# A graph layer and a two-expert feed-forward: the expert stage put into a hand-written order, with the turning of a later group behind layer two

## The chip, the cores and the metric

One NeuronCore of a Trainium2 chip runs the whole program. The metric is the time of one execution on the device in microseconds (us). Its engines are named as in the profile: PE multiplies matrices (PEld is its loading of weights), DVE and ACT are the vector and the scalar engine, POOL is GpSimd, and SP issues transfers (SPq is its queue of instructions). Each engine has its own list of instructions; a semaphore holds an instruction back until another engine, or a transfer, has done what it needs.

## The reference

The input is `x` with 6250 rows of 256 numbers, and a list of 206,250 edges. A graph convolution with a residual comes first; behind it stands the part that matters here, a layer norm and a feed-forward of two experts out of eight, chosen once for all rows:

```python
x = x + gnn(layernorm(x), edges)
# feed-forward on xf = layernorm(x), shape (6250, 256)
h = gelu(einsum('nd,edf->enf', xf, W1) + b1)      # 256 -> 512, exact gelu
y = einsum('enf,efd->end', h, W2) + b2            # 512 -> 256
out = einsum('ne,end->nd', w_dense, y)            # two experts have weight, top_k = 2
out = layer_norm(out + xf, gamma, beta)
x = x + out
```

## The kernel before

The 6250 rows lie in 49 tiles of 128 rows. The first two thirds of the time are the graph convolution; it ends with `x1_d`, the rows before the second layer norm, in device memory, and with the mean and the reciprocal deviation of each row, `mean2` and `rstd2`. A router then picks the two experts and loads their weights (`w1_sb`, `w2_sb`; `w2_sb` and the second bias are scaled by the routing weights on DVE, lines 1231 to 1238).

The stage of the experts goes over 13 **groups**: group 0 has one tile, the twelve others have four (`TN = 4`). A group passes through these steps:

- `take(i)` (line 888) allots three tiles and issues one transfer on SP (line 898), 512 KB of `x1_d` into `xt`. The tiles `yt` and `xt` come from a pool with `AH + 3` = 6 buffers each, `xT2` from one with `AH + 1` = 4; `AH = 3`.
- `turn(i, ps_x, eng)` (line 903) normalizes: for each of the four tiles one instruction (line 910, on DVE for groups 3 and up) writes `yt` from `xt`, and two PE transposes (line 915) put it into the PSUM tile `px`. Two ACT copies (line 917) take `px` to `xT2`.
- `biases(i)` (line 919) adds the second bias to `yt` and `beta` to `xt`, two POOL instructions (lines 922 and 925).
- `layer_1(i)` (line 1252) makes eight tiles `p1` in PSUM (two experts, four blocks of 128 hidden units), each by matmuls over the two halves of 256 columns (line 1261; each shows as two PE instructions, 32 for a group), and ACT takes each through gelu into `hT` (line 1265). `ps_1` has three buffers for `p1`.
- `layer_2(i)` (line 1269) makes, for each of the four tiles, one `p2` over both experts (line 1282; 16 PE instructions for a tile, 64 for a group). Behind it stands a chain on DVE and ACT for the tile: add `yt` (line 1287), the statistics of the last layer norm (1288, 1289), add epsilon (1291), square root on ACT (1292), subtract and scale by gamma (1294), reciprocal (1297), scale and add `xt` (1298). SP then stores the tile (line 1301).

Up to the stage, `take`, `turn` and `biases` have already run for groups 0, 1 and 2. In the stage ten turns are left, those of groups 3 to 12.

What sets the order: the part of the program under `tc.manual_schedule(engines={PE, DVE, ACT, SP, POOL})` (the convolution, and line 930 on, up to the scaling of the weights) has each engine's instructions in the order in which they are written. The stage of the experts, from line 1244, is not under it: there a planner in the framework puts each engine's instructions into an order of its own when the program is built, and may set an instruction ahead of those written before it on the same engine. The written order of the stage is

```python
        layer_1(0)
        for i in range(len(groups)):
            if i + 1 < len(groups):
                layer_1(i + 1)
            if i + AH < len(groups):
                take(i + AH)
                turn(i + AH, ps_x, nc.vector)
                biases(i + AH)
            layer_2(i)
```

## Time and profile before

| | us |
|---|---|
| three runs: median (lowest to highest) | 1150.8 (1148.29 to 1150.85) |
| the profiled execution | 1151.31 |
| its span, first to last instruction | 1149.2 |
| PE busy in the span | 1090.8 (95%) |
| DVE, ACT, POOL busy | 721.5, 623.1, 539.0 |
| PE busy from 795.60 to 1149.20, a stretch of 353.60 | 346.02 |
| DVE, ACT, POOL busy in that stretch | 129.56, 116.63, 56.00 |

The span is what lies between the first and the last instruction of the execution; the 2.1 us between 1149.2 and 1151.31 lie around it. "Busy" is the time in which an engine works on an instruction. The stage of the experts fills the last third of the span, from about 786 us. In the rows of the timeline a bracket at the end says how long the engine stood idle ahead of the row, and what ended that. The column PEclk is the clock that PE was granted, as a share of the full one.

### The profile page before, as it was taken

How to read it: one execution, taken by the hardware profiler on the slowest of the kernel's cores; microseconds unless marked ns; L12 is line 12 of the kernel's file. 1: busy time of each engine (PE TensorE's matmuls, PEld its weight loads, DVE VectorE, ACT ScalarE, POOL GpSimd, SP SyncE). 2: the span in 40 equal slices, each digit the busy share in tenths (PEclk: the TensorE clock that was granted, in tenths of full speed). 3: DMA queues.
4: the chain of work that ended last, by engine and by line, in shares of the span. 5: the costliest groups of instructions: out<-in, count | busy, mean ns of one | idle time of the engine just before them, and what ended most of it. 6: DMA issues, size and time to landing. Idle time of an engine off the chain costs nothing. (4 is left out here: it accounts for less than half of the span.)

```text
span 1149.2 us, 17869 instructions
## 1 busy us (share of the span) xinstructions
PE 1090.8 (95%) x6552; PEld 836.3 (73%) x6552; DVE 721.5 (63%) x1523; ACT 623.1 (54%) x1529; POOL 539.0 (47%) x473
## 2 busy tenths in 40 slices
PE   6977999999999999999999999885999999999997
PEld 5766788878888888788888888763566666666666
DVE  6878876867777877777777778745333333322335
ACT  3786466766766666676667666522533333333330
POOL 3713246777767676777666766425411111100000
PEclk9997899999999999999999999886999999999999
DMA  8709637676767777677777777534011111100001
GB/s 261 237 24 343 196 86 198 160 189 172 196 172 185 179 174 182 176 180 180 184 177 177 180 182 174 140 92 140 23 37 37 37 37 37 37 19 18 19 19 37
DMA packets 102750, 152.04 MB, mean 132 GB/s; under 512 B 10047, under 2 KB 48671, under 8 KB 102655
## 3 DMA queue, kind: packets, MB, share of 16 engines
q0 software_dynamic: 54080, 99.35, 35.3%
q1 hardware_dynamic: 45378, 48.93, 13.0%
q10 hardware_dynamic: 3196, 2.55, 0.8%
q8 instruction: 53, 0.87, 0.3%
q14 instruction: 43, 0.34, 0.1%
HBM read 123.42 MB, written 27.37 MB: 131 GB/s over the span
## 5 line engine op out<-in xcount | busy, mean ns | idle before, releaser
L737 POOL DMA_INDIRECT rows<-hl_d,g_src x360 | 409.5, 1137 | 221.7 <-PE pg L775 104.6
L644 PE MATMUL po<-hp,a_t 128*128 128x512 f32 x1911 | 481.8, 402 | 0.8 <-ACT a_t L628 0.8
L644 PEld LDWEIGHTS po<-hp,a_t 128*128 128x128 f32 x1911 | 351.9, 190 | 70.2 <-ACT a_t L628 1.0
L628 ACT CAST a_t<-pa 128x392 fp32r<-128x392 f32 x624 | 257.8, 502 | 218.0 <-PE pa L624 216.5
L455 DVE TENSOR_TENSOR unit<-iota,loT 128x2048 bf16<-128x2048 bf16 x156 | 190.4, 1221 | 51.3 <-PE pa L624 51.3
L1261 PE MATMUL p<-xT,w_sb 128*128 128x512 f32 (+2 forms) x416 | 173.0, 577 | 1.6 <-ACT xT L917 1.6
L1282 PE MATMUL p<-w_sb,hT 128*128 128x256 f32 (+1 forms) x784 | 171.2, 379 | 0.0
L1282 PEld LDWEIGHTS p<-w_sb,hT 128*128 128x128 f32 (+1 forms) x784 | 147.9, 190 | 20.8 <-issue 0.9
L624 PEld LDWEIGHTS <-unit 128*128 128x128 bf16 x2496 | 124.1, 100 | 49.0 <-issue 24.8
L624 PE MATMUL pa<-unit 128*128 128x98 bf16 x2496 | 148.6, 212 | 9.5 <-DVE unit L455 5.6
L455 DVE TENSOR_TENSOR unit<-iota,keyT 128x1568 bf16<-128x1568 bf16 x156 | 150.8, 967 | 0.0
L1261 PEld LDWEIGHTS p<-xT,w_sb 128*128 128x128 f32 x416 | 79.6, 200 | 88.2 <-issue 82.9
L1287 DVE TENSOR_TENSOR yt<-yt,p 128x256 f32<-128x256 f32 (+1 forms) x49 | 20.6, 421 | 179.6 <-PE p L1282 179.6
L756 ACT ACTIVATE oh_g<-iota_f,g_dst 128x128 fp32r<-128x128 f32 x360 | 123.9, 423 | 0.0
L1265 ACT ACTIVATE hT<-p,b_sb 128x512 f32<-128x512 f32 (+2 forms) x104 | 67.3, 660 | 82.9 <-PE p L1261 82.7
L775 PE MATMUL pg<-rows,oh_g 128*128 128x512 f32 x360 | 106.0, 392 | 1.6 <-DMA rows<-hl_d,g_src 1.6
L1292 ACT ACTIVATE rs<-rs 128x1 f32<-128x1 f32 (+1 forms) x49 | 9.9, 203 | 150.0 <-DVE rs L1291 150.0
L925 POOL TENSOR_TENSOR xt<-xt,beta_bc 128x1024 f32<-128x1024 f32 (+1 forms) x13 | 29.5, 2274 | 130.0 <-DVE yt L910 130.0
L775 PEld LDWEIGHTS pg<-rows,oh_g 128*128 128x128 f32 x360 | 68.1, 189 | 18.4 <-DMA rows<-hl_d,g_src 3.7
L922 POOL TENSOR_TENSOR yt<-yt,b_sb 128x1024 f32<-128x1024 f32 (+1 forms) x13 | 29.6, 2273 | 89.7 <-PE px L915 80.4
L758 ACT ACTIVATE oh_g<-oh_g 128x384 fp32r<-128x384 f32 (+1 forms) x140 | 67.1, 479 | 4.4
L679 DVE RECIPROCAL rstd<-rstd 128x1 f32<-128x1 f32 (+1 forms) x49 | 8.0, 164 | 88.2 <-ACT rstd L678 88.2
(183 smaller groups left out, 777.1 us busy)
## 6 DMA issues: line engine op xcount, KB each, us to landing
hl_d<-hp SPq DMA_DIRECT2D x7, 1792.0 KB
x_d<-x SPq DMA_DIRECT2D x49, 128.0 KB
xt<-x_d SPq DMA_DIRECT2D x12, 512.0 KB
out_dram<-yt SPq DMA_DIRECT2D x48, 128.0 KB
rows<-hl_d,g_src POOLq DMA_INDIRECT x360, 3.8
xb<-in_x_dram SPq DMA_DIRECT2D x6, 896.0 KB
xs<-in_x_dram SPq DMA_DIRECT2D x39, 128.0 KB
xg<-in_x_dram SPq DMA_DIRECT2D x9, 128.0 KB
```

Source lines behind the costliest of these rows:

```text
L455: nc.vector.tensor_tensor(oh, iota2[:, :m, :].unsqueeze(1).to_broadcast([P, HG // 2, m, 2]), v[:, s].rearrange("p (q t) -> p q t", t=2).un ...
L624: nc.tensor.matmul(pa[:, i].rearrange("p j h -> p (j h)"), oh_lo[:, q, :, t], oh_key[:, q, :, t], start=True, stop=True,)
L628: nc.scalar.copy(tiles[n][:, :, b * 2 * BG : (b + 1) * 2 * BG], pa.rearrange("p i j h -> p h (i j)"),)
L644: nc.tensor.matmul(pouts[n].rearrange("p k d -> p (k d)"), tiles[n][:, g, :], hp2[g // TB][:, g % TB].rearrange("p k d -> p (k d)"), start ...
L737: nc.gpsimd.indirect_dma_start(out=g_rows[j], out_offset=None, in_=hl_d, in_offset=bass.IndirectOffsetOnAxis(ap=g_src[:, j // GC, j % GC : ...
L756: nc.scalar.activation(oh[:, i, :], iota_f, AF.Abs, bias=g_neg[:, g, c : c + 1])
L758: nc.scalar.activation(oh, oh.bitcast(F32), AF.Relu, scale=-1.0, bias=1.0)
L775: nc.tensor.matmul(pouts[n].rearrange("p k d -> p (k d)"), oh[:, i, :], g_rows.pop(g * GC + c), start=False, stop=(c == GC - 1),)
L922: nc.gpsimd.tensor_tensor(yt[:, :nt, :], yt[:, :nt, :], b2_sb.unsqueeze(1).to_broadcast([P, nt, D]), OP.add)
L1261: nc.tensor.matmul(p1[:, :cols], w1_sb[:, e, k, f * P : (f + 1) * P], xT[:, k, :cols], start=(k == 0), stop=(k == ND - 1),)
L1265: nc.scalar.activation(hT[:, e, f, :cols], p1[:, :cols], AF.Gelu, bias=b1_sb[:, e, f : f + 1])
L1282: nc.tensor.matmul(p2[:r], hT[:, e, f, t * P : t * P + r], w2_sb[:, e, f, :], start=(e == 0 and f == 0), stop=(e == TOP_K - 1 and f == NF ...
```

## The change

The pools get one more buffer each (7 for `yt` and `xt`, 5 for `xT2`), the stage is put under the manual schedule for all five engines, the transfer of a group is issued one iteration earlier, and the turning and the biases stand behind `layer_2` in place of ahead of it.

```diff
-    xp = ctx.enter_context(tc.tile_pool(name="xp", bufs=AH + 3))
+    xp = ctx.enter_context(tc.tile_pool(name="xp", bufs=AH + 4))
...
-        xT = hp.tile([P, ND, TN * P], F32, name="xT2", bufs=AH + 1)
+        xT = hp.tile([P, ND, TN * P], F32, name="xT2", bufs=AH + 2)
...
     with ExitStack() as ph:
+        ph.enter_context(tc.manual_schedule(engines={PE, DVE, ACT, SP, POOL}))
         op_ = ph.enter_context(tc.tile_pool(name="op", bufs=3))
...
+        take(AH)
         layer_1(0)
         for i in range(len(groups)):
             if i + 1 < len(groups):
                 layer_1(i + 1)
+            if i + AH + 1 < len(groups):
+                take(i + AH + 1)
+            layer_2(i)
             if i + AH < len(groups):
-                take(i + AH)
                 turn(i + AH, ps_x, nc.vector)
                 biases(i + AH)
-            layer_2(i)
```

## The prediction

> **What bounds the kernel now.** I read the chain of work that ended last first, in the stretch of the stage. Columns: start, length, engine and line, how many instructions.

> ```profile
> 795.68 17.60 PE p L1261 x52
> 813.28 0.76 PE px L915 x7
> 814.04 3.46 PE p L1282 x16
> 817.50 13.73 PE p L1261 x32
> 831.23 0.87 PE px L915 x8
> 832.11 13.81 PE p L1282 x64
> 845.92 13.73 PE p L1261 x32
> ```

> From 795 us on the chain is PE alone, and piece follows piece without a hole: layer one 13.73 us, the eight transposes of a turn 0.87, layer two 13.81 to 13.82, so 28.42 a group. The clock is granted in full from 799 us to the tail. So no reordering of the other engines can gain anything in the steady part; it can only open holes in PE's row. PE's order is already the written one (layer one of the next group, turn, layer two).

> The second view is the timeline of DVE at a line 910 and around the end of a layer two (at 845.92).

> ```profile
> 824.55 1.38 DVE L910 TENSOR_SCALAR yt<-xt,mean,rstd 128x256 f32<-128x256 f32 x4 [4.61 <-DMA xt<-x_d]
> ...
> 845.96 0.42 DVE L1287 TENSOR_TENSOR yt<-yt,p 128x256 f32<-128x256 f32 x1 [1.18 <-PE p L1282]
> 846.42 0.43 DVE L1288 BATCH_NORM_STATS2 st<-yt 128x6 f32<-128x256 f32 x1
> ...
> 847.56 0.16 DVE L1297 RECIPROCAL rs<-rs 128x1 f32<-128x1 f32 x1
> 847.75 0.49 DVE L1298 SCALAR_TENSOR_TENSOR yt<-yt,rs,xt 128x256 f32<-128x256 f32 x1
> ```

> The chain of the group's last tile ends at 848.24, which is 2.32 us after PE has left layer two. Line 910 runs elsewhere: twelve of them between 794 and 811 us (the turns of groups 3, 4 and 5), the four at 824.55 belong to group 6, while PE turns group 4 only at 831. The planner keeps DVE two turns ahead of PE, and its 4.61 us wait for the transfer holds up nobody.

> The third view is PE's timeline where the stage begins.

> ```profile
> 785.81 2.93 PE L1261 MATMUL p<-xT,w_sb 128*128 128x128 f32 x12 [1.65 <-ACT xT L917]
> 795.21 0.48 PE L915 MATMUL px<-ident_r,yt 128*128 128x128 f32 x1 [6.47 <-DVE yt L910]
> 795.48 4.93 PE L1261 MATMUL p<-xT,w_sb 128*128 128x128 f32 x22
> ```

> The planner put one transpose of group 3 into the middle of layer one of group 0. Its DVE instruction stood behind the scaling of `w2_sb`, so PE stood idle for 6.47 us with 20 of group 0's 32 matmuls and all of group 1's behind it. It also shows that PE does not pass a waiting transpose.

> **What it adds: a wait at each turn.** In written order DVE's list is: the chain of all four tiles of group i, then line 910 four times for group i+3. PE's list is layer two of i, the eight transposes, layer one of i+2. The transposes need line 910, line 910 stands behind the chain of the last tile, and that chain needs the last matmul of layer two. Queued behind the transposes is all of layer one. Counted from layer two's end at 845.92: chain ends +2.32 (848.24), gap to the next DVE instruction 0.05 (as between other rows), four line 910 at 1.38 to 849.67, 0.05 from DVE to PE (795.16 to 795.21 in the chain), the last pair of transposes 2 × 0.87 / 8 = 0.22, so layer one starts at 849.94 in place of 845.92 + 0.87 = 846.79 by the chain. That is 3.15 us; reckoned by issue (layer one's first matmul shows at 845.76 already, its weights drawn ahead) it is 3.31. I take 3.3, bounds 3.1 and 3.6 (transposes at half clock: a pair took 0.69 at 782 us). Ten turns: 33 us.

> **What the wait does to the clock.** Steps of the granted clock lie at 768.25, 788.73, 792.14 and 798.97, all multiples of 3.41 us apart, so I cut PE's time at that grid (window: length, PE busy, clock).

> ```profile
> 112.89:116.30 3.41, 1.94 (x28) 1.00 1.03 376
> 116.30:119.72 3.42, 2.48 (x29) 0.50 1.03 381
> 232.36:235.77 3.41, 2.46 (x11) 1.00 0.77 183
> 730.70:734.12 3.42, 0.00 (x0) 1.00 0.70 164
> 734.12:737.53 3.41, 3.17 (x22) 0.50 0.19 59
> 737.53:740.94 3.41, 3.41 (x10) 0.50 0.00 0
> ```

> A window with 1.94 us of work is followed by half clock, one with 2.46 is not, and it comes back after a full window only: 3.17 us did not do. The new hole lasts from layer two's end to 4.0 us later, with only scattered transposes in it; however the grid lies, one window has at least 2 us of hole, so I expect the clock to fall at every turn. If the grid cuts the hole φ after its start, and φ is over 1.4, the clock falls there, the next window holds the rest of the hole and is not full, and the third brings it back at φ + 6.83; PE works at half speed from 4.0 to then and loses (φ + 2.8) / 2, 2.1 to 3.1 us. With φ below 1.4 it falls a window later and loses 1.4 to 1.7. A group then takes 28.42 + 3.3 + loss; at a loss of 2.4 that is 34.13, ten windows, so φ stays where it is (1.9), and from another φ each turn brings it halfway there. I take 2.4 a turn, 24 us for ten; the bounds are 0 (the clock is full now, so it can't gain) and 3.1.

> [...]

> **What it removes.** The early transpose of group 3 leaves layer one of group 0: PE goes on at 788.74, and the 20 matmuls (0.215 each by 52 in 17.60 less 32 in 13.73) end at 793.0, so layer one of group 1 ends at about 806.8 in place of 813.28: minus 6.5 us. Bounds 0 (expert 1's `w1_sb`, whose landing the trace does not show, comes as late as the second bias at 792.05 and the rest of the start slips with it) and 6.5; the weights were issued ahead of that bias at 779 to 780 us at some 350 GB/s, so I take 6.5. DVE's wait for `xt` (4.61 us in this row) goes too, but no one waited for it.

> **What is moved at no cost, and its cover.** *SP:* ten transfers of 512 KB as before, 0.4 us of issue each, now ahead of the group's four stores; SP waits on line 1298 for most of the stage, and a transfer that landed within some 4 us has over 50 us before its turn. Without that cover: 4.6 us a turn. Two transfers, not three, now run beside the weights. *ACT:* the two copies (1.07 us) stand behind the four square roots and end at about 851.2, the first `p1` of the next layer one is ready at 851.9, table load 1.28 and gelu 0.69 end at 853.8; PE needs that buffer for its fourth `p1`, three times 1.72 after 849.94, at 855.1. Cover 1.3 us, and more at half clock; without it, its excess is paid at each turn. *POOL:* the two additions (2.35 us each) run in layer one, when DVE is idle; next to POOL's work at 794 to 811 twelve line 910 took 16.57 us, four of them 5.5 in place of 1.38, so without that cover a turn would wait 4.1 us longer. The buffers add no instruction. The tail (layer two of groups 11 and 12, the last chain, the store) is unchanged.

> **Sum.** Against the profiled execution, 1151.3 (span 1149.2 and 2.1 around it, 0.5 above the median): 33 + 24 − 6.5 = +50.5, so 1202.

> **Rivals.**
> 1. *The stall without the clock.* If the short transposes count as work and windows of over 2 us still hold the clock: 1151.3 + 33 − 6.5 = 1178. For it: 2.46 us was enough at 232.36. Against: the hole leaves 1.4 us or less in its worse window. 10%.
> 2. *The start gives nothing back.* Stall and clock as above, expert 1's weights late: 1208. With 3.6 and 3.1 a turn besides, 1218. 8%.
> 3. *The other side: DVE is not held.* If line 910 still gets ahead of the last chain, transposes find `yt` ready, only the start's gain remains: 1151.3 − 6.5 = 1145. This decides as soon as the wait and the clock together cost under 0.65 us a turn. For it: line 910 needs nothing from layer two. Against: under the same schedule the router's DVE and PE rows (941, 945, 953, 969; 948, 956, 1215, 915) stand in written order throughout. 3%.
> 4. *The change does not do what it says* (the planner's order survives, early transpose included): 1151. 2%.

> **How the numbers follow.** The forecast has 77%, with its own range 1193 to 1210 (a loss of 1.5 a turn, or no gain at the start). The range 1180 to 1211 leaves out most of rival 1, the far end of rival 2, and 3 and 4. A measurement here tells about 0.3% from no change: faster 3%, within 2%, slower 95%.

> **What would show it.** Right: in each of ten groups PE idle some 2.8 us ahead of line 915, released by DVE line 910, whose four rows start right behind a line 1298; clock 0.50 for one or two windows after it; starts of layer one 34 us apart; no 6.47 us wait at 789. Wrong: line 910 ahead of line 1287 in DVE's row (rival 3), spacing of 31.7 us (rival 1), or ACT, not DVE, releasing PE.

## The result and the profile after

Slower: 1187.05 us median of four runs (1185.05 to 1190.03) against 1150.82 (1148.29 to 1151.28), a ratio of 1.0322 with a 95% interval of 1.0293 to 1.035. The profiled execution took 1190.03, its span is 1187.8, 38.6 us over the span of before.

The waits of PE in the stage come first (releaser, us in total, times, longest), then the chain that ended last over two turns.

```profile
PE px L915 <- DVE yt L910: 27.9, 10, 2.8
```

```profile
865.78 13.83 PE p L1283 x64
879.63 0.43 DVE yt L1288
...
881.42 0.48 DVE yt L1299
882.38 1.32 PE px L915 x8
883.70 13.73 PE p L1262 x32
897.43 13.83 PE p L1283 x64
...
914.03 1.57 PE px L915 x8
915.59 15.07 PE p L1262 x32
```

(Lines from 1246 on have moved down by one to three: layer one's matmul is line 1262, layer two's 1283, the last chain's ends are 1288 and 1299.) The chain was PE alone before; now it leaves PE at the end of each layer two, runs through the whole DVE chain of the last tile and through line 910, and comes back to the transposes. Layer two is as long as before. Layer one is 13.73 us in one group and 15.07 in the next. The timeline of DVE at the turn of group 4 shows what the transposes wait for:

```profile
848.17 0.48 DVE L1299 SCALAR_TENSOR_TENSOR yt<-yt,rs,xt 128x256 f32<-128x256 f32 x1
848.57 1.37 DVE L910 TENSOR_SCALAR yt<-xt,mean,rstd 128x256 f32<-128x256 f32 x4
```

Line 910 starts as line 1299 ends, with no bracket of idle time. Its transfer was no hindrance: SP issued it before 786 us. Only the place of line 910 in DVE's list is late. PE's first transpose follows at 849.12.

Where the 38.6 us went, by the chain's rows of before and after:

| | us |
|---|---|
| ten holes from layer two's end to layer one's start (4.78, 4.33, 4.09, 4.33, six of 4.08 to 4.09), 42.1, less ten turns of 0.87 | +33.4 |
| layer one over 13.73 (0.50, 1.37, 1.34, three of 1.70; four of none) | +8.3 |
| start: layer one of group 0 to the end of layer one of group 1, 785.81 to 813.28 before, 789.48 to 810.05 after | −6.9 |
| up to the start of the stage, where the program is the same: 785.81 to 789.48 | +3.7 |

The last row is no part of the change. In the profiled executions of the experiments below, but for the sixth, which alters the start, layer one of group 0 starts anywhere from 784.5 to 788.8 us, and 1190.03 is the slowest of the four runs. Without that row the sum is 34.8; the medians differ by 36.2, and the 1.4 us between the two stay unexplained.

Of the first row some 1.2 us belong to the clock: at three turns (holes of 4.78, 4.33 and 4.33 in place of 4.08) the transposes ran at half clock. So the wait by itself cost 32.2 us, and the clock 9.5, of which layer one lost 8.3.

The third view is PE's time cut at the grid on which this execution's clock steps lie, whole multiples of 3.41 us apart (window: length, PE busy with the number of instructions, clock; then the share of the DMA engines and GB/s).

```profile
812.35:815.76 3.41, 1.15 (x6) 1.00 0.00 0
815.76:819.17 3.41, 2.84 (x10) 0.50 0.51 145
819.17:822.59 3.42, 3.42 (x9) 1.00 0.14 47
...
846.48:849.89 3.41, 0.77 (x6) 1.00 0.11 34
849.89:853.31 3.42, 3.42 (x8) 0.50 0.50 159
877.20:880.61 3.41, 2.40 (x12) 1.00 0.11 38
880.61:884.03 3.42, 1.65 (x10) 1.00 0.29 58
884.03:887.44 3.41, 3.41 (x10) 1.00 0.39 134
...
945.47:948.88 3.41, 1.62 (x10) 1.00 0.26 60
948.88:952.29 3.41, 3.41 (x6) 0.50 0.43 137
```

After a window with 0.77 us of work the clock was 0.50 in the next one, and 1.00 after that one. 1.62 us was followed by 0.50, 1.65 by 1.00. At six of the ten turns the clock fell for one window, after one with 0.72 to 1.62 us of work. At four the hole is split more evenly over two windows, the emptier of which holds 1.63 to 1.91 us of work, and the clock stayed.

### The profile page after: what moved, and what is told of

Read it like the earlier page. It is cut to its first block, busy times and chain, and to the rows that moved or that the text cites. A ratio compares the mean times of both kernels' runs of the same rounds, so it can differ in the third digit from the quotient of the medians.

```text
span 1187.8 us, 17879 instructions
## 1 busy us (share of the span) xinstructions
PE 1105.4 (93%) x6552; PEld 839.5 (71%) x6552; DVE 708.5 (60%) x1523; ACT 624.2 (53%) x1529; POOL 540.2 (45%) x473
## 5 line engine op out<-in xcount | busy, mean ns | idle before, releaser
L1262 PE MATMUL p<-xT,w_sb 128*128 128x512 f32 (+2 forms) x416 | 181.2, 598 | 1.7 <-ACT xT L917 1.6
L1288 DVE TENSOR_TENSOR yt<-yt,p 128x256 f32<-128x256 f32 (+1 forms) x49 | 20.7, 422 | 259.7 <-PE p L1283 259.7
L384 PE MATMUL p<-w_sb,xT 128*128 128x256 f32 x196 | 49.2, 396 | 3.5 <-ACT xT L376 3.3
```

Source lines behind the costliest of these rows:

```text
L384: nc.tensor.matmul(p[:, t], xT[:, t, k, :], w_c[:, k, :], start=(k == 0), stop=(k == ND - 1),)
L1262: nc.tensor.matmul(p1[:, :cols], w1_sb[:, e, k, f * P : (f + 1) * P], xT[:, k, :cols], start=(k == 0), stop=(k == ND - 1),)
```

## The experiments

The theory: PE waits at each turn because line 910 stands behind the last chain in DVE's list, and some of the waits empty a clock window. The rivals: PE's own new order is at fault (transposes behind layer two), or the manual schedule, or the longer fetch; and the long layers one are not the clock. All but the seventh are edits of the changed kernel, and each is set against runs of the kernel before on the same chip (median 1151.25 for the first four, 1152.22 for the others).

### Line 910 alone moved back

`norm` is the loop over line 910, taken out of `turn`.

```diff
+            if i + AH < len(groups):
+                norm(i + AH, nc.vector)      # the four line 910 of turn()
             layer_2(i)
             if i + AH < len(groups):
-                turn(i + AH, ps_x, nc.vector)
+                turn(i + AH, ps_x, None)     # transposes and copies
                 biases(i + AH)
```

> Line 910 alone goes back ahead of layer two on DVE; the transposes, the ACT copies and the biases stay behind layer two, the transfer stays four ahead. If the ten waits come from line 910 standing behind the last tile's chain, no PE wait ahead of the transposes is left, the clock stays at 1.00 from the start of the stage to the tail, and the time is the kernel before less the start's gain of 6.9 us: 1144 (1142 to 1147). If the place of the transposes behind layer two is itself what costs (they follow p2's banks, or the copies come late for ACT), it stays within 5 us of the changed kernel: 1182 to 1190.

Measured: 1144.43, ratio 0.9943 (0.9925 to 0.9961). The chain is PE alone again, in the new order (line 1290 is layer two, 922 the transposes, 1269 layer one):

```profile
827.56 13.81 PE p L1290 x64
841.37 0.87 PE px L922 x8
842.24 13.74 PE p L1269 x32
```

Four DVE instructions a turn are all that the loss hangs on; with them ahead of layer two the change is a small gain, 6.8 us.

### The manual schedule left out

```diff
-        ph.enter_context(tc.manual_schedule(engines={PE, DVE, ACT, SP, POOL}))
```

> The changed kernel's text without the manual schedule: PE's order is still layer one, layer two, transposes, but the planner orders DVE. If only DVE's order matters, the ten waits vanish and the early transpose of group 3, which the planner again puts into layer one of group 0, costs its 6 to 7 us at the start: 1151 (1148 to 1154). If PE's new order is at fault, 1182 to 1190.

Measured: 1151.44, ratio 0.9999 (0.9983 to 1.0014). PE's list is the changed kernel's but for the transpose of group 3, yet it never waits at a later turn: the planner put sixteen line 910 ahead of the first chain (first row, DVE). At the start stands the old wait, now 5.45 us (second row, PE):

```profile
794.73 19.89 DVE L910 TENSOR_SCALAR yt<-xt,mean,rstd 128x256 f32<-128x256 f32 x16
...
795.59 0.48 PE L915 MATMUL px<-ident_r,yt 128*128 128x128 f32 x1 [5.45 <-DVE yt L910]
```

### Spare matmuls in the hole

The diff is shortened: the matmuls stand in a helper, and the tile `spare` takes one of the three buffers of `p2`.

```diff
             layer_2(i)
             if i + AH < len(groups):
+                for _ in range(6):
+                    nc.tensor.matmul(spare, ident, w2_sb[:, 0, 0, :], start=True, stop=True)
                 turn(i + AH, ps_x, nc.vector)
```

> The changed kernel with six spare matmuls of 256 columns (into a PSUM tile that nobody reads, for which p2 has two buffers in place of three) between layer two and the transposes: 6 x 0.43 = 2.6 us of PE work inside the hole of 2.8 us. If the clock is lost because a 3.4 us window holds under some 1.63 us of work, the clock stays at 1.00 in all ten turns, the waits stay, and the time falls by the 8.3 us that layer one lost: 1179 (1176 to 1181). If the longer layers one have another cause, or the spare work only delays the transposes: 1186 or more.

Measured: 1177.54, ratio 1.0245 (1.0219 to 1.0271). The chain at a turn (line 1270 is layer one, 1291 layer two, 1296 the chain's first):

```profile
1018.33 13.83 PE p L1291 x64
1032.18 0.43 DVE yt L1296
...
1034.92 1.32 PE px L915 x8
1036.24 13.73 PE p L1270 x32
```

The turn itself is as late as ever (4.08 us from layer two's end to layer one here), for the chain on DVE sets it. But each window at a turn now holds at least 3.1 us of work, the clock is 1.00 in all of them, every layer one takes 13.73 to 13.74, and the median falls by 9.5 us: the 8.3 that layer one had lost, and the 1.2 of the transposes at half clock. So the long layers one were the clock, and work in the hole kept it. Whether the filling of the windows or the length of the idle time decides, this run can't tell, as the longest idle time ahead of the transposes shrinks too, to 0.2 us; the last experiment bears on that.

### The whole turn back ahead of layer two

```diff
-            layer_2(i)
             if i + AH < len(groups):
                 turn(i + AH, ps_x, nc.vector)
                 biases(i + AH)
+            layer_2(i)
```

> The changed kernel with the whole turn and the biases back ahead of layer two, manual schedule and fetch four ahead kept. By the DVE theory line 910 runs within the first 5 us of layer one, PE never waits at a turn: 1144 (1142 to 1147), the same as with line 910 alone moved. If the manual schedule itself or the longer fetch distance costs, it lies above 1150.

Measured: 1144.94, ratio 0.9956 (0.9939 to 0.9973), the same as with line 910 alone (0.5 us apart). So the place of the transposes is worth nothing either way.

### Line 910 behind the chain, for the next turn

```diff
         layer_1(0)
+        norm(AH, nc.vector)
...
             if i + AH < len(groups):
-                turn(i + AH, ps_x, nc.vector)
+                turn(i + AH, ps_x, None)
                 biases(i + AH)
+            if i + AH + 1 < len(groups):
+                norm(i + AH + 1, nc.vector)
```

> Line 910 stays behind layer two and its last chain on DVE, as in the changed kernel, but for the group one later, so that the transposes behind layer two read what DVE wrote one iteration before. If what costs is that PE needs line 910 at once, no wait is left: 1144 (1141 to 1148). If standing behind the chain costs by itself, or the two POOL additions, which now run beside line 910 (DVE's four took 5.5 us there in the kernel before), hold PE up, PE waits at each turn and the time lies between 1150 and 1190.

Measured: 1143.63, ratio 0.9926 (0.9907 to 0.9944), with no PE wait at any turn: layer two, transposes and layer one follow each other without a hole.

```profile
823.36 13.81 PE p L1290 x64
837.17 0.87 PE px L922 x8
838.05 12.02 PE p L1269 x28
```

Line 910 stands where the change put it; it is only no longer needed at once. What costs is not a place behind the chain but one behind the chain with its reader next in PE's list. Two instructions on DVE were long here (line 1302 of that kernel, 0.47 us at 856.92, took 2.35 at 838.42, and line 1306, 0.48 at 857.57, took 2.38 at 840.87), and nobody waits for them. I take POOL's additions, due once the transposes end at 838.05, for the cause, which was not shown.

### The turn of group 3 at the very start

```diff
         take(AH)
+        turn(AH, ps_x, nc.vector)
+        biases(AH)
         layer_1(0)
...
-            layer_2(i)
-            if i + AH < len(groups):
+            if 0 < i and i + AH < len(groups):
                 turn(i + AH, ps_x, nc.vector)
                 biases(i + AH)
+            layer_2(i)
```

> The whole turn ahead of layer two, with the manual schedule (1144.9 where it was measured), but the turn and the biases of group 3 written ahead of layer one of group 0. PE then waits for DVE, which waits for the second bias and scales w2 first, with all 32 matmuls of group 0's layer one behind the transposes. If the start's gain is the planner's early transpose, this gives it back and more, as four line 910 and not one are waited for: 9 to 12 us over 1144.9, so 1154 to 1157. If the weights set the start anyway, it stays at 1145.

Measured: 1159.7, ratio 1.0066 (1.0048 to 1.0084): 14.8 us over 1144.94 (14.7 over the seventh experiment, which ran on the same chip as this one), and over the range that I gave. PE's timeline, and the row of DVE that it waits for:

```profile
797.62 0.66 PE L915 MATMUL px<-ident_r,yt 128*128 128x128 f32 x2 [9.61 <-DVE yt L910]
799.88 0.69 PE L915 MATMUL px<-ident_r,yt 128*128 128x128 f32 x2 [1.60 <-DVE yt L910]
802.23 0.69 PE L915 MATMUL px<-ident_r,yt 128*128 128x128 f32 x2 [1.66 <-DVE yt L910]
804.58 0.69 PE L915 MATMUL px<-ident_r,yt 128*128 128x128 f32 x2 [1.66 <-DVE yt L910]
...
796.66 7.86 DVE L910 TENSOR_SCALAR yt<-xt,mean,rstd 128x256 f32<-128x256 f32 x4
```

The direction is as expected: what stands ahead of layer one at the start holds PE up until DVE has scaled `w2_sb`. The size was off, as I read these rows, since I left out POOL; no run takes POOL away, so the cause is not shown. Its additions for groups 0 to 2 begin at 795.03, and four line 910, 1.37 to 1.38 us when alone, took 7.86: PE's last two steps of 2.35 us are those at which POOL's additions of 2.39 us start (797.28, 799.63, 801.99, 804.33).

### The manual schedule alone

The kernel before with one added line, old order, old buffers, fetch three ahead.

```diff
+        ph.enter_context(tc.manual_schedule(engines={PE, DVE, ACT, SP, POOL}))
```

> The kernel before with the manual schedule as its only edit: old order, fetch three ahead, old buffers. DVE's line 910 then waits for a transfer issued behind the stores of the group before, about 2.5 us into layer one, landed by 8 us, so it is done by 9.5 us and the transposes come at 13.7: no PE wait, 1144 to 1147. If the longer fetch and the added buffers matter, PE waits at the turns: each 1 us of wait gives 10, so 1155 or more.

Measured: 1145.0, ratio 0.9948 (0.993 to 0.9967), the same as with the added buffers and the early fetch (1144.94). DVE waits for its transfer here, and PE does not:

```profile
843.77 1.38 DVE L910 TENSOR_SCALAR yt<-xt,mean,rstd 128x256 f32<-128x256 f32 x4 [4.22 <-DMA xt<-x_d]
```

So the one useful part of the change is that the planner no longer orders the stage, 7.2 us; fetching earlier buys nothing, as line 910 ends at 845.15 and the transposes start at 850.97, 5.8 us later.

### One spare matmul

The third experiment with `range(1)`.

> The changed kernel with one spare matmul (0.43 us) in the hole (p2 with two buffers). A look at the clock rule alone: of the 3.4 us windows that hold the hole, those with under 1.6 us of PE work lose the clock in the next window, those with over 1.7 keep it; some of the ten turns, not all, lose it. The time lies between the changed kernel and the one with six spare matmuls: 1179 to 1187. If the clock is lost by the length of the unbroken hole, it is kept in all ten, as the hole is then 2.3 us.

One execution, 1187.82: just over the range that I gave, and not to be told from the changed kernel. Five of the ten turns lost the clock, and layer one lost 7.6 us there, against 8.3 in the changed kernel. The first rows are windows of PE, the last two its timeline at two turns that follow each other.

```profile
876.04:879.45 3.41, 1.06 (x8) 1.00 0.12 38
906.76:910.17 3.41, 2.75 (x13) 1.00 0.11 38
910.17:913.59 3.42, 1.73 (x10) 1.00 0.26 58
...
975.03:978.44 3.41, 1.66 (x10) 1.00 0.22 62
...
1039.88:1043.29 3.41, 1.62 (x10) 1.00 0.16 47
...
1041.67 1.31 PE L915 MATMUL px<-ident_r,yt 128*128 128x128 f32 x8 [2.35 <-DVE yt L910]
1075.01 1.32 PE L915 MATMUL px<-ident_r,yt 128*128 128x128 f32 x8 [2.35 <-DVE yt L910]
```

Half clock followed the windows with 1.06 to 1.62 us of work, full clock those with 1.66 and up. One window, the first (811.19, 1.55 us), kept the clock against this, and I can't say why. The length of the hole did not decide: with 2.35 us of unbroken idle time the execution lost it at one turn (1041.67) and kept it at the next (1075.01).

## Why the prediction was right, and where its sizes were off

The direction and the mechanism held. 1187 lay inside the wide range, 1180 to 1211, but outside the forecast's own, 1193 to 1210, which had been given 77%: it is 15 us below the forecast of 1202 and 9 above the first rival (1178), by one term.

1. *The wait at each turn* was right. Forecast 2.8 us of PE idle ahead of the transposes, released by line 910 right behind a line that ends the last chain; measured ten waits of 2.78 to 2.83. The cost of 33 us came out as 33.4, or 32.2 without the transposes at half clock. The first and fifth experiments show that it is line 910's lateness and nothing else.
2. *The clock* was the term that was mis-sized: 2.4 us a turn, 24 in all, forecast; 9.5 measured. Two parts of that step failed. "However the grid lies, one window has at least 2 us of hole", so that the clock falls at every turn, counts the transposes as hole and takes the fall to start at 1.94 us of work, from the window at 112.89, which holds bf16 matmuls. The eight transposes are 1.3 us of work, and with this stage's f32 work the clock fell after windows of up to 1.62 us and stayed at four turns, which had 1.63 to 1.91 us in the emptier window and lost nothing. Why the window at 112.89 fell at more work stays open. "The next window holds the rest of the hole and is not full", so that the clock would stay down, was wrong as well: the window from 815.76 held 2.84 us and full clock followed it. A row of before said so already, which the prediction passed over for the one with 3.17 us:

```profile
785.32:788.73 3.41, 2.92 (x12) 0.50 0.78 230
788.73:792.14 3.41, 0.01 (x1) 1.00 1.04 329
```

So a turn lost at most one window, 1.7 us, not 2.1 to 3.1. With that the steady spacing of ten windows that I derived fell too: the starts of layer one alternate, at last between steps of 31.65 and 33.34 us.

3. *The length of the idle time* did not decide on the clock: it fell at turns with 2.78 to 2.83 us of idle time (six times) and stayed at turns with the same 2.78 us (four times), by the filling of the windows.
4. *The start* gave back 6.9 us for 6.5 forecast. The second, fourth and seventh experiments bear it out: 1151.44 with the planner's early transpose, about 1145 without. It was the planner's transpose that had cost it, and the weights of the second rival did not take it back. The working had a slip: 52 matmuls in 17.60 us less 32 in 13.73 leave 0.194 us for each of the 20, not 0.215, and with that the forecast is 6.9. That it then meets the measured 6.9 so closely is partly chance, as the clock rose at 798.97 before and at 795.29 after.
5. *The moves at no cost* cost none: in the first and fifth experiments transposes, copies and biases stand behind layer two and PE has no hole at a turn. The earlier fetch was worth nothing, as said, which the seventh shows.
6. *The rivals.* The stall without the clock (1178) is just what the third experiment built, at 1177.5, and four of the changed kernel's ten turns went that way. The other side (1145) is what came out as soon as line 910 was not held up, at 1144. Neither is what the change as a whole did.

A version that beats both kernels is there: the turn in written order with line 910 in time, in any of four ways, at 1143.6 to 1145.0, 0.4 to 0.7% under the kernel before; the shortest is the manual schedule alone.

## What to carry to other kernels

Under a hand-written order, look on each engine for the producer of what the critical engine needs next, and read what stands ahead of it in that engine's list: here four instructions of 1.4 us, which needed nothing from layer two, cost some 32 us of waiting, and 9.5 more by the clock, since a chain that starts only when PE has finished stood ahead of them. Give such work a whole iteration of lead, either by writing it ahead of the stage that feeds the chain or by doing it for the next round. And before rewriting an order by hand, look for the one place where the planner's order hurts: it was a single transpose at the start, worth 6 to 7 us.

## What the runs showed of the chip

At idle times of 2.78 to 2.83 us layer one lost 0.50 to 1.70 us at six turns and nothing at four, by how the windows divided them, and spare work in the hole was worth its place: six matmuls a turn that compute nothing took 9.5 us off the time.
